# First and last tile: four products in full precision, nine unread products at a norm, and a new written order

## The chip, the cores and the metric

The kernel runs on one core of one Trainium2 chip. The metric is the device time of one execution in microseconds (us). TensorE is called PE, VectorE DVE, ScalarE ACT, GpSimd POOL and SyncE SP. SP issues almost all the DMA transfers here. "Granted clock" is the share of full speed that the chip's throttle allows PE, as the profile records it.

## The reference, cut to what matters

The input x is 32 sequences of 256 tokens of 128 features. Two layers follow each other; each is `x = x + s(xn) * silu(f(xn))` with `xn = layernorm(x)`.

```python
xs = jnp.pad(x, ((0, 0), (1, 0), (0, 0)))[:, :-1]        # first layer, s
xm = x * time_mix + xs * (1.0 - time_mix)
k = jnp.exp(jnp.minimum(jnp.einsum('btc,dc->bdt', xm, Wk), 60.0))
v = jnp.einsum('btc,dc->bdt', xm, Wv)
r = jnp.einsum('btc,dc->btd', xm, Wr)
wkv = _depthwise_causal_conv(k * v, w, T, C)             # decaying sums over time
wk = _depthwise_causal_conv(k, w, T, C) + 1e-09
s = jnp.einsum('btc,dc->btd', jax.nn.sigmoid(r) * (wkv / wk), Wo)
```

Beside it, the first layer's gate `f` is three products with weights of +1 and -1 (128 to 512 to 512 to 128 features) with relu. The second layer's `s` is a state space block (projection, convolution over 4 tokens, scan), and its `f` is a mixture of 2 shared and 16 routed experts with the 4 best weighted by a router.

## The kernel before

The tokens are cut into 16 tiles of 512 (two whole sequences each), named 0 to 15 (in base 36, 0 to f, in the written order). A tile lies as 128 features by 512 tokens. About two tiles are in flight at a time, the first layer of one beside the second layer of the tile before.

**Products.** Nearly all PE products are made from two rounded parts. A value is copied into a rounded type (fp32r) as its high part (`hi_of`, an ACT copy or activation), the rest is subtracted out as the low part (`lo_of`, on DVE or POOL), and `mm3` (L636) adds three products, high by high, low weight by high, and high weight by low. Weights are split once, by `halves` and in `w_o`. An unrounded product of fp32 operands is one call and becomes two passes through PE; the seven last `down` products of each tile are of this kind (tile `pm`, weight `w_n`).

**One tile's first layer.** `norm0` gives `xn`; `part0` splits it (`x1`); `mix` makes `xm` with DVE and splits it (`xm0h` by ACT, `xm0l` by POOL for tile 0). `key`, `kv` and `recept` multiply it by three of the four weights in `wkvro` (tiles `pk`, `pv`, `pr`). `quot` (L876) divides the two sums, multiplies by the gate `tr`, and splits the result (`z0h` by ACT, `z0l` by DVE). `back` (L910) multiplies by the output weight `w_o` (tile `po`), by the gate `g` of the signed products (`sign0`, `sign1`, `sign2`: tiles `pha`, `phb`, `pz`), adds onto `xr` and transposes to `pt`. `norm1` (L932) takes the statistics of `pt` on DVE (`bsb`, `mvb`), the power on POOL, normalises four blocks (`xnb`), transposes each back on PE (`psb`), and splits the result into `x2`, for tile 0 `x20h` and `x20l`. All of the second layer reads `x2`: `conv` and `res` (`pi`, `pres`), the router's `logits` (`pl`, eight small products), and `up` (`pu`).

**At the start** `warm` (L491) issues 14 products of a constant of ones, `wm`, whose results nothing reads, between the loads and the first transposes.

**What sets the order.** Every step is a generator; one step usually issues one instruction. `ORDER` (L160) is a string of three characters a step, the tile and the number of the part, and `run` (L334) takes the steps in that order. It thus fixes the sequence of every engine's queue, SP's DMA queue too; each queue is worked in sequence, with waits on semaphores. `SLOTS` (L106) says which buffer each new tile takes. PSUM has 8 banks, tag `psq`, one for each product tile.

Of the kernel before, what the change touches and what calls it, by code (L numbers as in the profile page):

```python
# [16 lines left out]
P = 128  # L17
# [3 lines left out]
NJ = NTOK // P  # L21
# [21 lines left out]
N1D = ()  # L43
NCV = 2
# [7 lines left out]
WARM = 14  # L52
WV = (1,)
# [54 lines left out]
        '0123045678250312530171120573663507222367502257603220367566275301132570002713511573207735201330152711'  # L108
        '357206635027117026535263170'
    ),  # L110
    'bs': '00000101110000011111101000000000',
# [4 lines left out]
        '0123401221043210301243011043210424013240043210433104231001324103031423011023410220143201120341021204'  # L116
        '3120102341022103421001243103'
    ),
    'h': (
        '012341056789abc5147603ac167459b82def9f2d5fe89417cb6a30gd48ac84d7g23b9f51915fb193604827gdca4cag8c54d7'  # L120
        '2063bf9171736190afb42d8g5cb8b248c5gd71a963f07d63d7g849b25c0fa1b99c5b48d3f6g71a02a20172ag639fd85c4be4'
        'f3c53f90ga21674ff47624fa8b19g05c3e1b1c5b2697f48ae30gdb3d0ed345g8f679c18c96cba817f05dg416'
# [3 lines left out]
    'md': '00000000000000',  # L126
    'mr': '0123032330203020032303030332',
    'mt': '00000000000000',
    'mv': '01111020345512202334455112225555',
    'pb': '0000000000000000',  # L130
    'psq': (
        '0123410532610762151760432154257262016421360403546030127013755147531650250435453743502615376542325635'
        '5753521073136243242133567061627674711474103462732241025402151603761476713733521354075716274030762700'
        '4561460135170171251324756562403123012105370657246247120643475127161340041041556237265737431704011604'
        '2056241673213723576060417245472522043734110723756356236247104323156315753653271534161721672027526342'
        '6405161501767261530175276374267743035134723640622474501664673701272140251706307130235045041507620543'
        '7316236723023754745104604303663025467375102130252312413657025302164301037637441270463527141026134571'
        '0012572743160732457347563'
    ),
    'rest': '0000000000000000',  # L140
    'rs': '01101010101010100101100110010110',
# [3 lines left out]
        '0120201210331200456721389046509183462920504382631594807461390470825a23481018973273991307128628531064'  # L145
        'a15037951a05430697341a87260489a3b0b63649623b0961257a3498c6892a756c68657a60b836a79543a584b890a3589c20'
        'b7240b5373b025053b78a504a2b580738b403a7283c9c4a09538c4537907c389405a6943ca2b65c4539b6935c2ab53c9b738'
        'a4c9057ba9874830b4a97b33b0296875920b657b989075a842b7653c1616c518474b42714812b0220021847b58451058501b'
    ),
    've': '0011111000000001000110111111111111',  # L150
    'wk': '00000000000000000000000000000000',
    'x2': '01100110011001100110011001100123',
    'xi': '01101010011001100110011010010110',
    'xna': '00',
    'xr': '0123454012354012',
# [5 lines left out]
g0pg0pg0pg0pg0p000g0hg0fg0pg0fg0fg0fg0fg00g0fg07g08g01100g0pg03002002002g0pg0fg0fg0gg0gg0hg04002g0og0o002g0g002002002g0g  # L161
g0g002g0ig0i002002002102102102g0jg0j102102102102102102g02g0gg0ag09g0cg0fg0fg0fg0m002g0k002002g0b002002102002002200002g0q
g0f102004g0fg0mg0d003008005102g0q102004102g0j003g0l005008004g0eg0kg0og05g0kg0fg0f102004102102006006102102102005300g0vg06
005007007008g0j00800e00e00e10100g00g00600g00e009006g0j00e00900900700700e00f00fg0j10300i00i00i00i00a00a00a00a00a00a00900a
00a00a10300900900900920220220220220220210510500g201g0v00f20220200b00b00b00b00900900h301g0l40100140000cg0t00cg0t20200c00c
00c00c00c20200c00j10600h106g0u00j00b00a00b00b00b00h202g0l00j00bg0r00b00j10820220200cg0u00cg0r10510510710720200d00dg0tg0t
g0t108g0sg0t109109106202302g0s10700j00d00d00d30210400j10c00d30210810c00d30250030230230230230210400j00d00k30200j00l00l109
10600l40210a30210c40220200l00l10c30210730210910430210a10410a10910810cg0ng0n10910c50240210e10e40270040240240240230200l00l
00l50240210c00m00l00m10c10c10e00m00m00m00m00m00m00m10i10i10e00m10910910a50250260040210a50250250250210a10a10a10e00m50210e
10a00m00m00m00m00m00m00m00m00n10f10f20210i109g0n50200m10f20400n00o20300n30210j10900q00n00q10c00q00q00q00q00q00o00q01s01s  # L170
01s10j60200q00n20360200o01k60201k00q60201k80060260200q60260201100r01s10j60201101101860210i00r00n01801800r00r00r30201k00n
01o01c00r00r01c70201o00r00r10a01100r01801c01o01470200r01410g01100r10g01o00r00r01gg0ng0n10g00o01110b01c01400r00r00n00o01g
01g70200u70200r10g10b01410b70270270270270200u00r01g90000u70210b00o00t00t10h00t10d01510b00n01901d00o10b00n10b10h00n10b10d
10d10d01l00u01p01w00o10b01001w10h01w01000o00o00o10b01001001030310d10d01601310d10d10j00t10j00p01601h01630401a00p00p10k00p
01301380201e01701720620680200p10j01080201t01780210j01x00p01ma0001b20610j10l10l20401q10l10l00s00z00z00z00s00s00w01f00w10l
00v20420820601i00v00z00z10l00z00y00y10l10l01u20880210l80280280201w10m10m20701j20700y10m20710m20520500x00x10m10m10m20501n
01y10m10m01020801r01v20701020801z10m20502040201020i20410m20i20e20940240280290200x80210m10m40220920e90210m10m20i20i10m10m
20e90210m40220920e10m20c90220910m902902902902209209c0010o10n20e10o10n00z90220c902a0210n00za02a02a0220e00z10q10qb0010q10q
10q10q30320f10q20f10q20f10o10n20950102120910o20a20a20c40210o20a02110n10q10q10q10n20j10r20j02102120c40220c20c20c10r10r20c
02102120c20a11802120a20911820j40311802111811120c11111111c10r20911c11c11c40411k10r10o10r10r20a40311k02111o11o11k10r11o10r  # L180
11k10r10o20a20a10r11o10r11g11110r11g11g10r11s10r10n11g11s11s10r10o11411411120g20g10r20g20a11111410r11s20b10n11420b20b115
20g10t20b11d20b20a20b20b20h11310n10n10n20b11911320h20b11l10t10t10u10u10u20h20b20d20d20d20d20d11610o10o10z10z10z10o11311t
10t11p20j11e10p11620j10u11w10p10p20j10p20d20d11w20d10p11611h20j11a11x11w20k11711711011020j20l20l20l10p11m11711w20l305305
30810s11b30530420l10s10s10z10w308305110110110a02a02a02a0211q10w30420l10v10y10y11i10v20l20l20l30e11f30820m30e20m30630610y
10x10x10z11y11010z50230811j50250230620m11u110502307307307a0230611n50220m20m20m20m20m20m11011r30720m11011vb0230420mb02b02
b0211z10x120a0220m20m30id0030i30930i30920m20m60120m20m20m30i30e30930e30a30a10z30e40410z10z30e30f30f20m50230c40430a30f30a
30930930c30930930c30c30c30930c12150230930c30c12120n20m12112120n30j12112130c20n30920o30c30j20o20n20o30a12120n20q20q20q20q
20q20q20q12120q21120o20q21121120q30j20o30a20q21k30a30a20n20r20r20r20r21k12140421o21o21k21s20r21c21k20o21s21s21o21121c21c
20o21s21g21c20r21g20r21820r20r20n20r21821121821420r21821420r20r21g20r21421130a30g30g21g30g20r21o30b30a20r30b30b20o20r214
30b30b30g30b20r21w21321w30b20n30h21321320o20o20t21520t20t30h20o21w21d20n20n30b30d30h20n21930d21l20t30d30d30j21t30j21030b  # L190
21030b30j20u50450330d20u20u21021021030d30d30j21630d21e21020u21h30j30l30l21630k40640621a21p30l30l40620z21x20z20z21640620p
21720p20p20p21720z20z30l20p21721b21m30l20p21i30l30l21u20s30l30m30m20w30m30m21f21j20s20s20w21q30m30m30m30m30m20y20y20v405
40520v21n21r30mc02c02405c0240521w40720y20x40760220x21y21v602602407b02602b02b02b02408c0240i40i20z210e0040821z40i407b02b02
21030m22060221040i20x40e70140930m30m40e40e30m30m30m30m40930m20z40840c40940e50430m30m20z20z40a40a40e40e60240c40c409408409
40940c40940c40c22122160240c40f40f40c40f40a40940c40a30o40922130o50422122122130n22150440j40a30n40j30n40940c30n30q30q30q221
30q30q30q30q30q30o40a40a30q30n40a30q30q30o30r40j30n30r30r30r31850322131c31c31831831c31131831131130n31k30o30r31o31o31o31c
31130r30r31k31k31k30r30r30n30r31s31s31s30r30r31430r30r31430o31431131g31o31g30r31g31131s40g40g40a30r40g30r30o31w31w31g40a
30r31w31440b40b40g40b40b31530o40b40b40b30t30n30n40b31d30n30t31331930t31l31330o30o40h30o31p31340d40h40d40d40d40b40h40j30u
# [98 lines left out]
def recurrent_d2(  # L297
# [439 lines left out]
    def mix(i):  # L737
# [18 lines left out]
        yield  # L756
        nc.scalar.copy(hi_of(s, "m", f"xm{i}", "xmp"), xm)
        yield
        lo_of(s, "m", f"xm{i}", "xmp", xm, "gpsimd")


    def sign0(i, m_):
# [169 lines left out]
    def norm1(i):  # L932
# [10 lines left out]
        for j in range(NJ):  # L943
# [10 lines left out]
            if j == 0:  # L954
                ps = bank([P, NJ, P], f"psb{i}", "psn")
# [427 lines left out]
```

## Time and profile before

| | us |
|---|---|
| three runs | 659.71, 660.61, 661.27; median 660.61 |
| the profiled execution | 659.82 |
| its span, first to last instruction | 658.0 |
| PE busy in the span | 641.4 |
| DVE busy | 572.2 |
| ACT busy | 549.3 |
| POOL busy | 384.0 |

The profile shows one execution. Its page gives the busy time of each engine and 40 slices of the span; the trace behind it can be asked for the instructions of an engine in order of time, for busy time in any stretch, and for the chain of waits that ended last. A number in square brackets at an instruction is the time its engine idled before it, with what ended the wait. Matmuls are pipelined, so that the distance of their starts, not their listed length, is what one costs.

### The profile page before, as it was taken

The page shows a single profiled execution, that of the slowest core. Times are in us where ns is not written, and L with a number is a line of the kernel's source. Part 1 is how long each engine was busy: PE and PEld are TensorE (multiplying, and loading weights), DVE is VectorE, ACT ScalarE, POOL GpSimd, SP SyncE. Part 2 cuts the span into 40 slices and gives each one's busy share as a digit, 9 for nine tenths or more (in the row PEclk, how much of TensorE's full clock was granted, in tenths as well). Part 3 has the DMA queues.
Part 4 walks back from the last instruction along what each step waited for, and adds up shares of the span by engine and source line. Part 5 has one row for each costly group of instructions (what it writes and reads, how often), then busy time and mean ns, then how long its engine had stood idle before and what let it go on. Part 6 is the DMA issues. An engine that isn't in the chain of part 4 may idle for free.

```text
span 658.0 us, 8819 instructions
## 1 busy us (share of the span) xinstructions
PE 641.4 (97%) x2626; PEld 461.5 (70%) x2626; DVE 572.2 (87%) x1364; ACT 549.3 (83%) x911; POOL 384.0 (58%) x398
## 2 busy tenths in 40 slices
PE   8999999999999999999999999999999999999997
PEld 6667676876757777576777767677675876767664
DVE  5989999979988899888888988988888798979886
ACT  8969797878969879797888979889797997967984
POOL 6585848567392773828466393944738374262542
PEclk9979999999999999999999999999999999999999
DMA  7334223142230413204132220413123040310431
GB/s 239 138 80 142 69 84 113 64 130 65 93 103 32 137 59 114 65 24 144 43 132 65 87 91 30 133 49 130 47 71 110 17 130 12 91 46 0 146 94 69
DMA packets 43648, 57.38 MB, mean 87 GB/s; under 512 B 3936, under 2 KB 20432, under 8 KB 43600
## 3 DMA queue, kind: packets, MB, share of 16 engines
q1 hardware_dynamic: 43456, 56.80, 26.9%
q8 instruction: 21, 0.34, 0.2%
q14 instruction: 27, 0.22, 0.1%
q10 hardware_dynamic: 144, 0.01, 0.0%
HBM read 52.02 MB, written 4.78 MB: 86 GB/s over the span
## 4 chain that ended last, share of the span: by engine, by line
PE 78%; DVE 11%; ACT 6%; issue 2%; DMA 2%; POOL 1%; SPq 0%; DVEq 0%; ACTq 0%
PE phb L634 15%; PE pm L634 14%; PE pu L634 13%; PE pc L634 6%; PE pha L634 4%; PE pz L634 3%; PE pi L634 3%; PE py L634 3%; PE pres L634 3%; PE pp L634 2%; PE po L634 2%; PE pk L634 2%; PE pl L634 2%; PE pv L634 1%; ACT L410 1%
## 5 line engine op out<-in xcount | busy, mean ns | idle before, releaser
L414 POOL TENSOR_TENSOR act<-act,ge 128x512 f32<-128x512 f32 x109 | 139.2, 1301 | 19.3 <-DMA ge<-gd 14.7
L410 ACT ACT_TABLE_LOAD x99 | 127.0, 1283 | 2.8 <-PEq L1371 1.2
L634 PE MATMUL pm<-act,w_n 128*128 128x512 f32 x224 | 106.0, 592 | 0.0
L417 DVE SCALAR_TENSOR_TENSOR pi<-xiz,par_sb,pi 128x512 f32<-128x512 f32 x96 | 70.4, 744 | 1.0 <-ACT pi L976 0.7
L414 POOL TENSOR_TENSOR xc_0l<-y,xc_0h 128x512 fp32r<-128x512 f32 x15 | 19.4, 1296 | 85.0 <-ACT y L411 64.3
L634 PEld LDWEIGHTS pm<-act,w_n 128*128 128x128 f32 x224 | 41.8, 189 | 29.9 <-issue 23.5
L411 ACT ACTIVATE act<-pu 128x512 f32<-128x512 f32 x109 | 61.2, 601 | 1.2 <-PE pu L634 0.3
L414 POOL TENSOR_TENSOR y<-y,rs 128x512 f32<-128x512 f32 x30 | 38.3, 1278 | 18.7 <-DVE y L1122 18.1
L1122 DVE TENSOR_TENSOR_SCAN y<-pd,y 128x256 f32<-128x256 f32 x64 | 39.9, 669 | 4.4 <-ACT pd L411 4.1
L414 POOL TENSOR_TENSOR xr<-gm,xr 128x512 f32<-128x512 f32 x15 | 19.3, 1288 | 30.1 <-DVE gm L414 25.1
L634 PE MATMUL phb<-ha_0h,w 128*128 128x512 f32 x64 | 27.3, 431 | 0.1
L1056 POOL MEMSET m<- 128x16 f32 x16 | 1.8, 112 | 43.7 <-DVE m L1054 43.7
L634 PE MATMUL phb<-ha_0l,w 128*128 128x512 f32 x64 | 26.1, 410 | 0.0
L634 PE MATMUL phb<-ha_2h,w 128*128 128x512 f32 x64 | 25.6, 403 | 0.0
L634 PE MATMUL phb<-ha_1h,w 128*128 128x512 f32 x64 | 25.5, 401 | 0.0
L634 PE MATMUL phb<-ha_3h,w 128*128 128x512 f32 x64 | 25.5, 398 | 0.0
L411 ACT ACTIVATE pd<-pd 128x512 f32<-128x512 f32 x32 | 17.9, 581 | 9.0 <-PE pd L634 8.8
L634 PE MATMUL phb<-ha_3l,w 128*128 128x512 f32 x64 | 25.3, 396 | 0.0
L634 PE MATMUL phb<-ha_2l,w 128*128 128x512 f32 x64 | 25.2, 397 | 0.0
L952 DVE TENSOR_SCALAR xnb<-pt,mvb 128x128 f32<-128x128 f32 x64 | 22.8, 401 | 2.3 <-POOL mvb L669 2.2
L634 PE MATMUL phb<-ha_1l,w 128*128 128x512 f32 x64 | 24.7, 396 | 0.0
L414 POOL TENSOR_TENSOR xc_1l<-y,xc_1h 128x512 fp32r<-128x512 f32 x15 | 19.4, 1296 | 8.7 <-ACT y L411 8.7
(1160 smaller groups left out, 2201.9 us busy)
## 6 DMA issues: line engine op xcount, KB each, us to landing
ge<-gd SPq DMA_DIRECT2D x128, 256.0 KB
mra<-mda SPq DMA_DIRECT2D x28, 256.0 KB
xt<-in_x SPq DMA_DIRECT2D x16, 256.0 KB
xr<-in_xr SPq DMA_DIRECT2D x16, 256.0 KB
out_x<-xr SPq DMA_DIRECT2D x16, 256.0 KB
w_up<-in_w_up SPq DMA_DIRECT2D x3, 192.0 KB
gd<-gT SPq DMA_DIRECT2D x16, 32.0 KB
w_n<-in_w_down SPq DMA_DIRECT2D x1, 448.0 KB
```

The lines of the kernel that those rows point to most:

```text
L410: nc.scalar.preload_act_table_set(SETS[kinds[0]])
L411: nc.scalar.activation(*args, **kw)
L414: getattr(nc, engine).tensor_tensor(o, a, b, op)
L417: nc.vector.scalar_tensor_tensor(o, a, s, b, op0, op1)
L634: nc.tensor.matmul(ps, lhsT=w, rhs=r, start=start, stop=stop)
L952: nc.vector.tensor_scalar(xn[:, j, :], s["pt"][:, j, :], mv[:, j, 0:1], r, ALU.subtract, ALU.mult)
L1056: nc.gpsimd.memset(m8[:, :, TOPK:8], -1.0)
L1122: nc.vector.tensor_tensor_scan(y[:, tok], sp[:, tok], y[:, tok], 0.0, ALU.mult, ALU.add)
```

## The change

For tiles 0 and 15 (`NAT`), `xm` and the quotient are no longer split: `key`, `kv`, `recept` and `back` make one product each from the unrounded values and the unrounded weights, where they made three. `wkvro` gets a place of its own, as it is read to the end. In `norm1` of tile 0, nine products of the constant `wm` are added, 128 by 128 by 128, into the bank of `psb`, read by nothing: six ahead of the four transposes and one after each of the first three.

`ORDER` and `SLOTS` are written anew from the first character to the last. Read out by queue, the new order differs from the old most in the first tile:

- SP: the first seven loads are `k0`, `xt` of tiles 0 and 1, `k2`, `w_dt`, `k1`, `wkvro` (before: `xt` of tile 0, `w_dt`, `w_rt`, `k0`, `xt` of tile 1, `wkvro`, `k2`).
- PE: 13 of the 14 unread products stand ahead of the first transpose (before 10); of the six new ones, one stands ahead of and five behind the last four `phb` products of tile 1 that come ahead of `norm1`'s transposes.
- ACT: the copy `w_k_h` moves from ahead of tile 0's first use of `psa` to behind its third relu; `w_c_h` moves from ahead of the gate `g0` to behind it; one more table load in the whole kernel (100, before 99).
- DVE: two subtractions and products of small constants (`w_r`, `cs`) move from the start to between two steps of tile 0's quotient; `ha1_1l`, `ha1_2l` and `xm1` stand between the quotient and `g0`.
- POOL: `w_c_l` moves from ahead of tile 0's `xr` addition to just ahead of the power in `norm1` of tile 0; two small weight steps (`w_p`) move from there to behind.

In the middle tiles the queues hold the same steps in nearly the same sequence, with neighbours exchanged. PE's queue still closes with tile 15's seven unsplit `down` products and the six `py`; between `pd15_0`, which tile 15's last scan waits for, and these stand two split `down` products (before, these two and two `pc`).

```diff
+NAT = (0, 15)
...
+WARM2 = 6
...
     def w_o(i):
-        w = cst("w_o", (P, P))
+        ready["w_of"] = w = cst("w_o", (P, P))
...
             stt(seqs(xm), seqs(xn), col(MIX), t1[:, :, 0:T], ALU.mult, ALU.add)
+        if i in NAT:
+            s["m"] = xm
+            return
         yield
         nc.scalar.copy(hi_of(s, "m", f"xm{i}", "xmp"), xm)
         yield
         lo_of(s, "m", f"xm{i}", "xmp", xm, "gpsimd")
+
+    def kvr(i, ps, k):
+
+        if i in NAT:
+            mm(ps, raw["wkvro"][:, k, :], st[i]["m"])
+        else:
+            w = ready["w_k"]
+            yield from mm3(lambda: ps, (w[0][:, k], w[1][:, k]), lambda: st[i]["m"])
...
-        yield ["mix", "w_k"]
+        yield ["mix", "get_wkvro" if i in NAT else "w_k"]
         pk = bank([P, NTOK], f"pk{i}", "pk")
-        yield from mm3(lambda: pk, (w[0][:, 0], w[1][:, 0]), lambda: s["m"])
+        yield from kvr(i, pk, 0)
...
         yield ["recept"]
-        if POC:
+        if POC and i not in NAT:
             stt(pv, s["tr"], 1.0, pv, ALU.add, ALU.mult)
...
-        if POC:
+        if POC and i not in NAT:
             w = ready["w_o"]
             yield from mm3(lambda: po, w, lambda: s["z"])
         else:
-            mm(po, ready["w_o"], s["tr"])
+            mm(po, ready["w_of"], s["tr"])
...
+        for k in range(WARM2 if i == 0 else 0):
+            yield
+            if k == 0:
+                ps = bank([P, NJ, P], f"psb{i}", "psn")
+            mm(ps[:, NJ - 1, :], wm[:, 0:P], wm[:, 0:P])
         for j in range(NJ):
...
             nc.tensor.transpose(ps[:, j, :], xn[:, j, :], ident)
+            if WARM2 and i == 0 and j < NJ - 1:
+                yield
+                mm(ps[:, NJ - 1, :], wm[:, 0:P], wm[:, 0:P])
...
-        ("wkvro", [P, 4, P], wkvro, "raw"),
+        ("wkvro", [P, 4, P], wkvro, None if NAT else "raw"),
```

## Prediction

> **What bounds the kernel now.** I read the page first, then busy time by stretch, PE's instructions in order of time around the slow slice, and the chain of waits at both ends.
>
> ```profile
> PE 641.4 (97%) x2626; PEld 461.5 (70%) x2626; DVE 572.2 (87%) x1364; ACT 549.3 (83%) x911; POOL 384.0 (58%) x398
> ...
> PE   8999999999999999999999999999999999999997
> ...
> PEclk9979999999999999999999999999999999999999
> ```
>
> PE is full in 38 of 40 slices, so a microsecond of PE work or of PE idling is about a microsecond of time. One slice, the third, has a low granted clock. By stretch (columns: PE, PEld, DVE, ACT, POOL busy, clock):
>
> ```profile
> 25.00:41.50 16.50, 13.74 (x55) 8.85 (x54) 15.42 (x52) 12.76 (x25) 14.83 (x19) 1.00 0.40 114
> 41.70:48.50 6.80, 6.80 (x21) 5.64 (x21) 5.19 (x18) 5.04 (x9) 4.75 (x6) 0.50 0.07 12
> 46.00:100.00 54.00, 53.08 (x217) 38.79 (x217) 52.88 (x148) 47.14 (x81) 33.06 (x36) 0.98 0.32 102
> 100.00:580.00 480.00, 475.65 (x1979) 345.42 (x1978) 421.20 (x968) 408.76 (x671) 287.34 (x268) 1.00 0.26 82
> 580.00:653.50 73.50, 71.95 (x277) 47.58 (x275) 61.53 (x141) 54.77 (x87) 31.55 (x31) 1.00 0.20 66
> ```
>
> For 6.80 us the clock is 0.50: 3.4 us of PE work are lost there. But from 46 to 100 us DVE is nearly as full as PE (52.88 of 54.00), so what PE wins early DVE need not follow. From 100 to 580 PE idles 4.35 us, to 653.5 another 1.55. PE at the fall of the clock:
>
> ```profile
> 38.79 0.40 PE L634 MATMUL phb<-ha_3l,w 128*128 128x512 f32 x1
> 39.54 1.28 PE L956 MATMUL psb<-ident,xnb 128*128 128x128 f32 x4 [0.35 <-DVE xnb L952]
> 41.50 0.67 PE L634 MATMUL pi<-x20h,w_i_h 128*128 128x512 f32 x1 [0.68 <-ACT x20h L959]
> ...
> 48.36 0.46 PE L634 MATMUL pu<-x20l,w_u_h 128*128 128x512 f32 x1
> 48.66 0.40 PE L634 MATMUL pu<-x20h,w_u_h 128*128 128x512 f32 x1
> ```
>
> Between 39.03 (0.24 after the start of the last `phb`) and 41.50 PE has four short transposes and nothing else, the second norm of tile 0. Then products start 0.43 us apart instead of 0.23, until 48.5. Five instructions of other engines in order of time, which the steps below use:
>
> ```profile
> 32.32 0.69 ACT L411 ACTIVATE g<-pz,cs 128x512 f32<-128x512 f32 x1
> 33.81 1.29 POOL L414 TENSOR_TENSOR xr<-xr,g 128x512 f32<-128x512 f32 x1 [0.26 <-DVE g L414]
> 37.72 0.19 POOL L667 TENSOR_SCALAR veb<-mvb 128x4 f32<-128x4 f32 x1 [0.41 <-DVE mvb L664]
> 45.85 0.29 DVE L1027 TENSOR_REDUCE lg<-pl 128x64 f32<-128x128 f32 x1 [1.61 <-PE pl L634]
> 48.75 1.37 DVE L1049 TENSOR_TENSOR pb<-lg,tot 128x64 f32<-128x64 f32 x1
> ```
>
> The chain of waits near its end (start, length, what):
>
> ```profile
> 646.04 6.01 PE pm L634 x14
> 652.04 1.41 PE py L634 x6
> ```
>
> DVE stood 1.61 us for the slow router products, and ACT 1.48 us behind it. In the chain, a pass of an unrounded product (`pm`) costs 6.01/14 = 0.43 us, and PE works without a gap up to the last `py`.
>
> **The change part by part.** The sum is made against the profiled execution, 659.82 us (span 658.0), which lies inside the three runs and 0.79 under their median 660.61; I carry the difference over to the median.
>
> *Four products.* Three rounded products cost 3 x 0.233 = 0.70 us of PE, one unrounded product 2 x 0.43 = 0.86: +0.16 each, +0.64 for a tile. Per tile two ACT copies of 0.5 us (`xm0h`, `z0h`), a POOL subtraction (`xm0l`, 1.35) and a DVE one (`z0l`, 0.60) go. In tile 0 PE idles 2.76 us between 25 and 41.5, so its +0.64 is taken as covered (without that cover, +0.64).
>
> *The way to tile 0's second norm.* From 10 to 31 us ACT is full, and its chain is what ends last. In front of `g0` the new queue loses `xm0h` (0.51, by the distance of the starts), `z0h` (0.57) and `w_c_h` (0.52), and gains `w_k_h` (0.40), which was issued earlier: 1.2 less. The start gives a little back: `k0` is loaded ahead of tile 0's `xt`, one issue of 0.47 us later, and the first weight chunk `w1` (0.71) stands ahead of `x10h` where `w_k_h` and `t1z` (0.40 and 0.58) stood. So `g0` starts about 1.1 earlier than 32.32. DVE's `g` follows it (it waited 0.32 for ACT before) as `z0l` is gone, and so does POOL's `xr`. On POOL `w_c_l` (1.29) now queues ahead of `veb`, and the norm waits behind it; but 0.74 of `w_p` has left that place, and 0.41 was idle: 0.14 later. The normalised blocks then come 1.0 us earlier.
>
> *w_r and cs on DVE's quotient chain.* They hold no more than 0.2 us, unless POOL reads SBUF then. The `pb` product above took 1.37 while POOL ran a 1.30 subtraction from the same moment, and the same instruction took 0.22 at 560.66; `cs` itself took 1.23 beside `xm0l`. So this move costs 0 to 1.0 us each; I take 0.3 for both, since DVE's `g` has 0.32 of waiting to lose first and half of POOL's work there is small.
> The Trainium skill (SBUF — State Buffer, "Who interferes with whom") has the rule behind it: a DVE instruction with both inputs in SBUF contends with a POOL instruction that reads SBUF, and the later one blocks for the whole of it. It speaks against putting these two there; by it both would block, about 2 us on this chain.
>
> *Nine unread products.* No row has them: two passes each of 128 columns. A 256-column pass of `pw` costs 0.21 us warm (4 in 0.79 of weight loads), an unrounded weight load 0.19, a transposing pass 0.11. So 0.22 to 0.38 each, 2.0 to 3.4 us in all. The gap they fill was 0.51 ahead of the first transpose, 0.2 after each of three, 0.68 before `pi`. PE reaches the five behind the last `phb` about 1.1 us earlier than before, if the chain above holds; they take 1.1 to 1.9, and delay the first transpose by 0 to 0.3 against the new `xnb`; each of the three between adds 0 to 0.2. Bounds for this edit: 0 to +1.9 (no lead at all and the upper price). I take +0.4, near the lower end since the lead is the likelier case. Together, `x20h` comes 0.3 to 0.4 us earlier (bounds: 1.1 earlier, 1.4 later).
>
> *The clock.* The new products put 2.0 us or more into a gap of 2.5. Between 24.5 and 27.9 us PE was idle for about 1 of 3.4 us and the clock stayed at 1.00; after the last product, at 653.43, it fell 3.1 us later. So with two thirds of the gap filled I expect it to stay. The low time, 6.8 us, is twice 3.4; the window in which it fell held 0.7 us of products and four transposes.
> The Trainium skill (TensorE: Matmul & The Clock Gate, Part 1) asks for a whole idle window of about 3.4 us before the clock is halved, which by itself would make the nine products needless, as no idle time here was over 0.7 us. Part 4 of the page adds that transposes do not count as busy, which would leave 2.5 us idle. By the page's rule alone the clock should not have fallen; the row shows that it did, and the row decides.
>
> What that is worth: PE's 3.4 us at most. But the router's way is x20l (ends 42.13), one `pi` and eight `pl` at full clock (0.23 + 0.80): 43.2, while DVE has `pk`, `hb_0l`, `hb_3l` and one `bsa` to do until 44.25. So `lg` comes forward by the 1.61 that DVE waited, and the stretch to 100 us, which DVE fills, by 1.6; DVE's remaining 1.1 us of idling there could add up to 0.8. I take -1.6 (bounds 0 and -3.4), plus the -0.3 of the way there: **-1.9**. What is late next is DVE.
>
> *Tile 15.* PE is full, so +0.64; but its norm chain left PE idle 1.13 us between 580 and 612, and it loses `z15h` and `z15l` (1.1 us). Bounds -0.5 to +0.64; I take **+0.2**.
>
> *The order.* In the middle the queues hold the same sequence with neighbours exchanged, and SP's gate loads too. PE idles 4.35 us there; half of that more or less is ±2. One more ACT table load is 1.28 us of an engine with 17% to spare. I take **0**. At the end PE's closing stretch after `pd15_0` is 0.23 + 0.47 + 6.01 + 1.17 before the last `py`: 7.9 us, against 7.2 that softplus, scans and `yy` took there from 644.86 to 652.1. It stays covered.
>
> Sum: -1.9 + 0.2 + 0 = **-1.7**. The profiled execution would be 658.1, the median **658.9** us.
>
> **The rivals.**
> *The clock falls anyway (slower).* The new quotient leaves PE idle between 25 and 31 us (it waited 0.84 and 0.62 before), and the unread products come too late or too short. For: 0.7 us of products in a window did not hold it. Against: the first unread products held the clock at 1.00 from the start. Then the 3.4 us stay lost, the nine products stand on the norm's way (+1.9 at the upper end, less 1.1 of lead), and tile 15 adds 0.64: +1.4, **662.0** us. It decides as soon as the granted clock around 42 us is 0.50.
> *DVE or a bank takes it all (no change).* The clock stays, but DVE meets POOL's reads in the quotient (+1.0 to 2.0), and later the order loses what is left: -1.9 + 1.5 + 0.2, **660.4** us. For: DVE's 52.88 of 54.00.
> *More is kept.* The whole 3.4 us and 0.8 of the way: about **656.6** us, if the new order has moved DVE work out of 46 to 100 us, where ACT and POOL have room.
>
> **How the numbers follow.** 0.2% is 1.3 us, about what a measurement of this kernel can tell from no change. Forecast 0.45 (657.6 to 660.0), more kept 0.15, no change 0.2, slower 0.2 (the clock case and an order that costs 2 us in the middle). Faster by more than 0.2% means under 659.3: most of the forecast, all of the third rival, 0.58. Same 0.2, slower 0.22. The range leaves out one tenth at each end: 656.3 to 662.0.
>
> **What would show it.** Right: clock 1.00 from 40 to 50 us, `lg` of tile 0 near 44 instead of 45.85, `g0` near 31.3, the third slice of PEclk at 9. PE's idle time from 100 to 580 near 4.4. Wrong: a 0.50 anywhere in 38 to 50, transposes of `psb` that start late behind the unread products, `w_r` or `cs` at over 1 us, or `pt` of tile 15 waiting longer than before.

## The result, and the profile after

The changed kernel is slower: 663.63 us, the median of six runs (661.92 to 664.03), against 660.75 for the kernel before (six runs). The ratio is 1.0040, 95% interval 1.0026 to 1.0055, which is 2.6 us. The forecast was 658.9 with a range of 656.3 to 662.0. The profiled execution of the changed kernel took 662.92 us (span 661.1). Below, kernels are compared by their ratio to the kernel before, run beside them on the same chip; 0.001 of it is 0.66 us.

The page of the changed kernel, its busy times, PE's row and the clock's row:

```profile
PE 645.3 (98%) x2636; PEld 459.1 (69%) x2636; DVE 569.7 (86%) x1362; ACT 548.4 (83%) x908; POOL 380.2 (58%) x396
...
PE   8999999999999999999999999999999999999997
...
PEclk9899999999999999999999999999999999999999
```

PE's busy time rose by 3.9 us, more than the span did (3.1). The dip of the clock has moved from the third slice to the second. Busy time by stretch (PE, PEld, DVE, ACT, POOL, then the clock), to be laid beside the rows of before:

```profile
25.00:41.50 16.50, 14.48 (x54) 9.95 (x53) 13.51 (x47) 11.59 (x22) 12.88 (x15) 0.90 0.33 98
41.70:48.50 6.80, 6.12 (x42) 5.34 (x41) 6.76 (x22) 5.33 (x11) 5.83 (x6) 1.00 0.11 39
46.00:100.00 54.00, 53.69 (x228) 39.14 (x227) 52.49 (x151) 48.81 (x84) 36.05 (x41) 1.00 0.32 104
100.00:580.00 480.00, 475.30 (x1961) 340.46 (x1960) 418.88 (x963) 405.93 (x668) 282.20 (x265) 1.00 0.25 81
```

The clock is at 1.00 where it was at 0.50, from 41.7 to 48.5, and from 46 to 100 us PE takes 228 instructions where it took 217. That part of the forecast came true in this execution. The loss shows in the last row, and it shows in the count more than in the busy time: from 100 to 580 us PE idles 4.70 us (before 4.35), but it takes 1961 instructions where it took 1979.

The end did what was forecast. In the chain of waits near its end (start, length, what), PE again works without a gap from `pm` to the last `py`:

```profile
648.71 6.47 PE pm L635 x16
655.18 1.40 PE py L635 x6
```

The way to tile 0's second norm did not. These are DVE, ACT and POOL instructions of the changed kernel in order of time; where an engine idled before one, the idle time and what ended it stand in brackets:

```profile
27.46 0.70 DVE L562 TENSOR_TENSOR w_r<-raw_w_rt,w_r 128x16 fp32r<-128x16 f32 x1
...
32.72 0.69 ACT L412 ACTIVATE g<-pz,cs 128x512 f32<-128x512 f32 x1 [0.24 <-PE pz L635]
...
38.31 1.28 POOL L415 TENSOR_TENSOR w_c_l<-w_x,w_c_h 128x512 fp32r<-128x512 f32 x1
40.32 0.20 POOL L668 TENSOR_SCALAR veb<-mvb 128x4 f32<-128x4 f32 x1 [0.73 <-DVE mvb L665]
...
43.99 0.59 ACT L977 CAST x20h<-psb 128x512 fp32r<-128x512 f32 x1 [1.47 <-PE psb L971]
...
47.12 0.29 DVE L1045 TENSOR_REDUCE lg<-pl 128x64 f32<-128x128 f32 x1
```

`g0` starts at 32.72, not at the 31.2 of the forecast. Only 0.24 us of that is a wait for PE's `pz`: the table load ahead of it on ACT ended at 32.48, and tile 0's first exponential, `kt`, had started 1.6 us later than before (17.59, before 15.97). `veb` comes 2.6 us later than before, and `x20h` at 43.99 where it had been at 40.86. From there the full clock wins 1.9 us back: `lg` is 1.3 later than before, not 3.1. Why `pz` was late shows in PE's instructions in order of time:

```profile
27.69 0.47 PE L635 MATMUL phb<-ha_0h,w 128*128 128x512 f32 x1 [0.91 <-DVE hb_2l L418]
...
28.89 0.50 PE L635 MATMUL phb<-ha_0l,w 128*128 128x512 f32 x1 [0.50 <-DVE ha_0l L418]
...
29.49 0.63 PE L635 MATMUL pz<-hb_0l,w 128*128 128x512 f32 x1
29.92 0.63 PE L635 MATMUL pz<-hb_1h,w 128*128 128x512 f32 x1
```

PE started five products between 26.2 and 29.4 us. There the clock fell to 0.50, until 32.8, and PE ran seven of the eight `pz` products at a distance of 0.43 us instead of 0.23: the clock had fallen earlier than in the kernel before, at the quotient.

By PE's own ledger (the distance of each start to the next, less what such an instruction takes in full flow) the added work is 3.2 us, 8 x 0.16 for the unsplit products and 18 x 0.107 for the unread ones, and the excess over it is 35.1 us in both kernels. It fell by 2.9 us up to 100 us and by 1.2 behind 580, and rose by 4.0 between. This looks as if the added work had simply been added, which is one theory; that the order lost in the middle what it had won at the start is another. The experiments tell them apart.

### The profile page after: what moved, and what is told of

It reads as the page before. It is cut to its first block, busy times and chain, and to the rows that moved or that the text cites. A ratio compares the mean times of both kernels' runs of the same rounds, so it can differ in the third digit from the quotient of the medians.

```text
span 661.1 us, 8827 instructions
## 1 busy us (share of the span) xinstructions
PE 645.3 (98%) x2636; PEld 459.1 (69%) x2636; DVE 569.7 (86%) x1362; ACT 548.4 (83%) x908; POOL 380.2 (58%) x396
## 4 chain that ended last, share of the span: by engine, by line
PE 79%; DVE 9%; ACT 8%; issue 2%; DMA 1%; SPq 1%; POOL 1%; DVEq 0%; ACTq 0%; POOLq 0%
PE phb L635 15%; PE pm L635 14%; PE pu L635 12%; PE pc L635 6%; PE pz L635 4%; PE pha L635 4%; PE py L635 3%; PE pres L635 3%; PE pi L635 3%; PE pp L635 2%; ACT L411 2%; PE po L635 2%; PE pk L635 2%; PE pl L635 1%; ACT act L412 1%
## 5 line engine op out<-in xcount | busy, mean ns | idle before, releaser
L635 PE MATMUL phb<-ha_0h,w 128*128 128x512 f32 x64 | 28.9, 454 | 1.0 <-DVE hb_2l L418 0.9
L415 POOL TENSOR_TENSOR xr<-xr,g 128x512 f32<-128x512 f32 x15 | 19.8, 1320 | 10.6 <-DVE g L415 10.6
L994 ACT ACTIVATE pi<-pi,par_sb 128x512 f32<-128x512 f32 x32 | 24.0, 754 | 0.5
```

The lines of the kernel that those rows point to most:

```text
L415: getattr(nc, engine).tensor_tensor(o, a, b, op)
L635: nc.tensor.matmul(ps, lhsT=w, rhs=r, start=start, stop=stop)
L994: nc.scalar.activation(pi, pi, AF.Identity, bias=col(CONVB + h), scale=col(cw + 3))
```

## The experiments

The written order is a sequence of steps, so two orders can be joined: the steps of one up to some point, then the steps that are left in the sequence of the other. Buffers were carried over with the part that they belong to. "Old" is the order of before without the steps that fall away.

| kernel | start / tiles 5 to 11 / end | unsplit | unread | ratio to before, 95% | us |
|---|---|---|---|---|---|
| after | new / new / new | 0, 15 | yes | 1.0040 (1.0026 to 1.0055) | +2.6 |
| e1 | old / old / old | 0, 15 | yes | 1.0031 (1.0017 to 1.0045) | +2.0 |
| e2 | old / old / old | none | yes | 0.9992 (0.9977 to 1.0007) | -0.5 |
| e3 | old / old / old | 0, 15 | no | 1.0027 (1.0012 to 1.0042) | +1.8 |
| e4 | new / new / new | 0, 15 | no | 1.0057 (1.0036 to 1.0078) | +3.8 |
| e5 | old / old / old | 0 | yes | 1.0004 (0.9992 to 1.0016) | +0.3 |
| e6 | old / old / old | 15 | yes | 1.0017 (1.0004 to 1.0030) | +1.1 |
| e7 | old / new / new | 0, 15 | yes | 1.0046 (1.0029 to 1.0064) | +3.0 |
| e8 | new / old / old | 0, 15 | yes | 1.0006 (0.9996 to 1.0017) | +0.4 |
| e9 | new / old / old | 0 | yes | 0.9985 (0.9972 to 0.9997) | -1.0 |
| e10 | new / old / old | none | yes | 1.0028 (1.0011 to 1.0045) | +1.8 |
| e11 | new, one step moved | 0, 15 | yes | 1.0052 (1.0032 to 1.0072) | +3.4 |
| e12 | new / new / new | 0 | yes | 1.0053 (1.0033 to 1.0073) | +3.5 |
| e13 | new / old / new | 0, 15 | yes | 0.9979 (0.9968 to 0.9991) | -1.4 |
| e14 | new to tile 8, then old | 0, 15 | yes | 1.0036 (1.0024 to 1.0048) | +2.4 |
| e15 | old / old / new | 0, 15 | yes | 0.9997 (0.9985 to 1.0008) | -0.2 |
| e16 | new, other PSUM banks | 0, 15 | yes | 1.0044 (1.0029 to 1.0058) | +2.9 |
| e17 | e13, other PSUM banks | 0, 15 | yes | 1.0004 (0.9989 to 1.0019) | +0.3 |
| e18 | new, one table load less | 0, 15 | yes | 1.0066 (1.0046 to 1.0085) | +4.4 |

### The edits apart from the order: e1, e2, e3, e4

```diff
 e1: ORDER, SLOTS: those of before, without the steps that fall away,
     and with nine steps of norm1 of tile 0 added
 e2: as e1, and
-NAT = (0, 15)
+NAT = ()
 e3: as e1 without the nine steps, and
-WARM2 = 6
+WARM2 = 0
 e4: the new ORDER without the nine steps, and
-WARM2 = 6
+WARM2 = 0
```

> The written order of before, with both edits of the work in it: four unsplit products in tiles 0 and 15 (the steps that fall away are struck out of the order) and the nine unread products (six ahead of tile 0's first psb transpose, one behind each of the first three). Theory 'order': the new order loses some 4 us between 100 and 580 us and the edits are worth what was forecast; then this kernel is at 659.0 us, 1.7 under before. Theory 'work': PE is the bound, and all PE work that the edits add shows (8 x 0.16 for the unsplit products, 18 passes of 0.107 for the unread ones, 3.2 us), whatever the order; then 663.9 us, as after. Theory 'clock': the gain hangs on where the clock falls; 659 with a granted clock of 1.00 from 40 to 50 us, 662 or more without.

> Before with the nine unread products alone, in the order of before. 'Order': the clock stays at 1.00 from 40 to 50 us, and the 1.6 us that the clock was put at come in, less up to 0.4 for the products' place on the norm's way: 659.0 to 659.5. 'Work': 18 x 0.107 = 1.9 us more PE work, 662.6. 'Clock': 659 if no slice near 41 to 48 us is at 0.50, 661 to 662.5 if one is.

> Before with the four unsplit products of tiles 0 and 15 alone, in the order of before. 'Order': the tile 0 products are covered and tile 15 costs 0.2; ACT loses two copies ahead of g0, so 660.0 to 661.0 with the low clock of before still there. 'Work': 8 x 0.16 = 1.3 us more, 662.0. 'Clock': as before, 660.7, the low clock moved by no more than 1 us.

> After without the nine unread products, its order otherwise. 'Order': the loss of the middle stays, so 663.0 or more, and 664 to 665 if the clock falls at tile 0's second norm without them. 'Work': 1.9 us less than after, 661.7. 'Clock': 663.6 if the low clock lies at 29 to 33 us as in after, since nothing before that time changes.

Measured: e1 662.31 us, e2 660.00, e3 661.65, e4 664.12, before 660.40. No theory fits all four. "Order" misses e1 by more than 3 us: the edits by themselves, in the old order, already cost 2.0 us. "Work" fits e3 (1.3 for a measured 1.8) and is 1.2 too high for e1, but it misses e2: the unread products add 1.9 us of PE work and make the kernel no slower. They hold the clock, as a stretch of e2's profile shows (columns as above):

```profile
41.70:48.50 6.80, 5.72 (x28) 4.38 (x28) 6.20 (x20) 6.65 (x12) 5.70 (x8) 1.00 0.17 39
```

The runs show besides how often the clock falls and what that costs. The kernel before was timed in 142 runs whose clock is listed: in 46 of them the mean granted clock is 0.991 to 0.996, in the other 96 it is 0.998 to 1.000. The means are 660.93 and 659.61 us. The fall thus costs 1.32 us (standard error 0.18), close to the 1.6 of the forecast, but it happens in a third of the runs; the profile that the forecast was read from, at 0.993, was one of that third. With the old start and the unread products (e1, e2, e5, e6, e7, e15), 4 of 65 runs are below 0.998, all of them e5's. So the edit is worth about 0.4 us on the mean. With the new start and the unread products (after, e8 to e14, e16 to e18) it is 48 of 106 runs; in the six profiles of these kernels that show a fall, one lies at the quotient, between 28 and 35 us, ahead of the unread products (e10 has another at 14 us). The new start thus brings a fall of its own, which they can't hold off.

e4 says the same from the other side: without the unread products the new order is 1.1 us slower than after (intervals overlapping), all six runs are below 0.998, and its profile has the fall behind tile 0's second norm, from 44.1 to 50.9 us.

### Which tile, and which half of the order: e5, e6, e7, e8

```diff
 e5: as e1, and
-NAT = (0, 15)
+NAT = (0,)
 e6: as e1, and
-NAT = (0, 15)
+NAT = (15,)
 e7: ORDER: old up to the first py of tile 5, then new
 e8: ORDER: new up to the first py of tile 5, then old
```

> The order of before with the nine unread products and unsplit products in tile 0 only. Its base is the kernel with the unread products alone, 660.0 us, whose clock never fell; both edits together stood at 662.3. Theory 'work': tile 0's four products add their 0.64 of PE and nothing covers it, 660.6. Theory 'cover', that of the prediction: PE idles in tile 0's first stage, so nothing is added, 660.0. Theory 'tile 0': the whole 2.3 us come from here, because tile 0's chain has no lead to lose, 662.3.

> The order of before with the nine unread products and unsplit products in tile 15 only. Base 660.0. 'Work': 0.64 more, 660.6. 'Cover': the forecast's +0.2, 660.2. 'Tile 15': the profiled kernels with unsplit products lost 1.2 to 1.4 us between 545 and 596 us, so this tile carries most of the loss, 661.3 to 662.0.

> All edits; the order of before up to the first py of tile 5 (about 280 us), and the new order from there on, the steps already taken left out. Base: all edits in the old order, 662.3. Theory 'middle': the new order loses its time between 340 and 440 us, so this kernel has the loss whole, 664.5 to 666. Theory 'start': the new order's loss is its start (tile 0's second norm 3 us later), and its rest is even with the old one, 662.3 or less.

> All edits; the new order up to the first py of tile 5, and the order of before from there on. 'Middle': without the stretch from 340 to 440 us of the new order, 661 to 662. 'Start': 663.5, as after.

Measured: e5 660.23 us, e6 661.18, e7 662.82, e8 660.09, before 659.78. Against e2, tile 0's unsplit products cost 0.8 us, near their 0.64 of PE ("work"), and tile 15's cost 1.7, more than twice their work. The two add up to e1. The traces don't put all of this at the edits. By the starts of the same PE instructions, e5 is 0.4 us behind e2 up to 100 us and 1.8 from 130 us on: between them, at 126 us, DVE is held up in the steps of a later tile (the race in the last section). e6 loses 1.1 us at the same place and 0.9 behind 560 us. e2's twelve times stand in two groups, 657.81 to 659.59 and 660.42 to 661.05, so prices taken against its median are rough.

Then the order: e8 is 1.7 us faster than e1, so the new start gains, although its `x20h` starts later than e1's (43.34, e1 42.27); and e7 is 1.0 slower than e1, so the rest of the new order loses. "Middle" was right in direction, though e7 fell short of its figure. Where the start gains is seen in DVE's rows, first e1, then e8:

```profile
157.52 1.75 DVE L418 SCALAR_TENSOR_TENSOR xm<-mra,par_sb,t1z 128x512 f32<-128x512 f32 x1
```

```profile
156.56 0.74 DVE L418 SCALAR_TENSOR_TENSOR xm<-mra,par_sb,t1z 128x512 f32<-128x512 f32 x1
```

The same PE instructions of e8 start 1.1 us behind e1 at 40 us and 1.4 ahead of it at 200, with steps of 0.75 to 1.0 us at 126, 158 and 194 us. At these three places e1's DVE takes 1.3 to 1.8 us for a `lg` or `xm` while POOL works, and e8's takes 0.2 or 0.7. From 40 to 200 us e1 has seven such rows of over 1 us, e8 one (e5 eight, e9 one). That these steps are the gain fits their sum; no run has tested it.

### A better kernel, and the longest wait: e9, e10, e11, e12

```diff
 e9: as e8, and
-NAT = (0, 15)
+NAT = (0,)
 e10: as e9, with tile 0's split steps put directly behind what they split, and
-NAT = (0,)
+NAT = ()
 e11: the new ORDER, with the first product of pha10_2 (a07) moved behind pt9's transposes
-a0681x81fa0781w80y
+a0681x81f81w80y
...
-c0290l80x80x81j
+c0290la0780x80x81j
 e12: the new ORDER with tile 15's split steps put directly behind what they split, and
-NAT = (0, 15)
+NAT = (0,)
```

> The new order up to the first py of tile 5, the order of before from there on; nine unread products; unsplit products in tile 0 only. Theory 'sum': the parts add up. With tile 15 unsplit as well it stood 0.4 us above before, and tile 15's unsplit products cost 1.6 (661.18 less 660.0, with the ratios' bases), so this kernel is 1.2 under before. Theory 'same': tile 15's loss is made up elsewhere when the start is early, so no change against the kernel with both tiles, 0.4 above before.

> As the last, but with split products in tile 0 too (the copies and subtractions put directly behind the values that they split, and the split of the first layer's weights ahead of tile 0's use of them): new start, old rest, nine unread products, nothing unsplit. 'Work': tile 0's unsplit products cost their 0.64 of PE, and this kernel is 0.6 faster than the last, 1.8 under before. 'Chain': in the new start ACT has no room for the copies, so it is 0.5 to 1 slower than the last, 0.2 to 0.7 under before.

> After with one step moved: the first product of pha10_2 goes from just ahead of tile 9's transposes pt9 to just behind them, and the two tiles exchange PSUM banks from there on, so that pt9 follows psb_8 (read early) and not pd8_1 (read by tile 8's scan, 0.9 us after the sum is ready and later). Theory 'bank': the wait of 1.97 us at pt9 goes, and 1 to 2 us with it: 661.6 to 662.6. Theory 'elsewhere': DVE or ACT are what is late there, the wait turns up again within 20 us, 663.3 or more.

> After with tile 15's four products split again (copies and subtractions directly behind the values that they split), tile 0 unsplit. 'Tile 15': the 1.6 us found in the old order come back here too, 662.0. 'Made for it': the new order's last stretch is laid out for unsplit products, so nothing comes back, 663.6.

Measured: e9 659.32 us, e10 661.81, e11 663.73, e12 663.69, before 660.62. e9 beats the kernel before, by 1.0 us. e10 is 2.8 us worse than e9, more than "chain" had. Two instructions of ACT show why, first e9, then e10:

```profile
17.57 0.62 ACT L413 ACTIVATE kt<-pk 128x512 f32<-128x512 f32 x1
...
43.95 0.59 ACT L978 CAST x20h<-psb 128x512 fp32r<-128x512 f32 x1 [1.47 <-PE psb L972]
```

```profile
19.47 0.59 ACT L413 ACTIVATE kt<-pk 128x512 f32<-128x512 f32 x1
...
45.99 0.59 ACT L978 CAST x20h<-psb 128x512 fp32r<-128x512 f32 x1 [1.49 <-PE psb L972]
```

The copies of the weights and of `xm0` that split products need hold tile 0's first product `pk` 1.2 us back (14.44, e9 13.27) and its first exponential 1.9, and the delay stays whole to `x20h`. In this execution of e10 a fall of the clock from 14.3 to 17.7 us adds to it; but in the runs without a fall the two kernels also stand 2.8 us apart (means 661.55 and 658.78). So tile 0's unsplit products cost 0.8 us where the order was made for split ones, and are worth 2.8 us where it was made for them. This price holds for the places that I gave the copies; better ones were not tried.

e11 took away the longest wait of the middle. In the changed kernel it looks so, first PE, then DVE:

```profile
385.47 0.80 PE L635 MATMUL pha<-x110h,w 128*128 128x512 f32 x1
387.67 0.41 PE L938 MATMUL pt<-ident,xr 128*128 128x128 f32 x2 [1.41 <-DVE y L1140]
...
384.86 1.48 DVE L418 SCALAR_TENSOR_TENSOR xm<-mra,par_sb,t1z 128x512 f32<-128x512 f32 x1
386.27 1.26 DVE L1140 TENSOR_TENSOR_SCAN y<-pd,y 128x256 f32<-128x256 f32 x2
```

`pha10_2` had been exchanged with `pt9` and took the PSUM bank that became free early; `pt9` had to wait for the bank of `pd8_1`, which tile 8's scan reads, and the scan queued behind `xm11` on DVE, which took 1.48 us beside POOL's products where the median `xm` of e13 takes 0.74. In e11 PE shows this:

```profile
385.15 0.38 PE L938 MATMUL pt<-ident,xr 128*128 128x128 f32 x2
386.69 0.27 PE L685 MATMUL pmva<-ident,mva 128*8 128x128 f32 x1 [1.15 <-ACT act L412]
...
387.44 0.50 PE L635 MATMUL pha<-x110h,w 128*128 128x512 f32 x1 [0.37 <-DVE ha_1l L418]
```

`pt9` starts 1.8 us earlier (2.5, less 0.7 that this execution was ahead), and the next taker of a bank, `pmva12`, waits instead, for a gelu behind a table load, and `pha10_0` after it: 1.15 and 0.37 for 1.41. The time did not move. "Elsewhere" holds: at this place moving the wait to another tile made no difference.

e12 gave nothing either (3.5 above before, after 2.6): where the end was laid out for unsplit products, splitting them again gains nothing.

### Where the new order gains and loses: e13, e14, e15

```diff
 e13: ORDER: new up to the first py of tile 5, old to the first py of tile 11, then new
 e14: ORDER: new up to the first py of tile 8, then old
 e15: ORDER: old up to the first py of tile 11, then new
```

> All edits; the new order up to the first py of tile 5, the order of before from there to the first py of tile 11 (about 515 us), the new order from there on. Theory 'own gain': the last stretch of the new order is 2 us better by itself (it is laid out for tile 15's unsplit products), so this kernel is 2 us faster than the one with the old order to the end, which stood 0.4 above before: 1.6 under before. Theory 'catching up': the new order only regains there what DVE and ACT had in hand because PE was late, so this kernel is 0.4 above before.

> All edits; the new order up to the first py of tile 8 (about 400 us), the order of before from there on. 'Early': the loss begins at 330 us and holds most of its sum by 400 (2.5 of 4 in the profiles), so 1.5 to 2.5 us above the kernel that changes at tile 5, 2 to 3 above before. 'Late or given back': what is lost to 400 us is regained later under the old order, under 1 us above before.

> All edits; the order of before up to the first py of tile 11, the new order from there on. Base: all edits in the old order, 2.0 above before. 'Own gain': 2 us less, even with before. 'Catching up': 2.0 above before.

Measured: e13 659.42 us, e14 663.15, e15 660.62, before 660.70. "Own gain" holds twice, with the new start (e13 against e8, -1.8) and with the old one (e15 against e1, -2.2). "Early" holds: e14 has 2.0 us of loss against e8. e13 is all of the change but for the middle of the order, and it is the fastest kernel of this study, 1.4 us under before (interval 0.6 to 2.1; e9 lies inside it). The change as it was made differs from e13 in the order of tiles 5 to 11 alone, and in the buffers that go with it, and that costs 4.0 us (about 2.8 to 5.2, the two intervals taken as independent). With the old start the same exchange, e7 against e15, costs 3.2. Busy time from 340 to 460 us, the changed kernel first, then e13:

```profile
340.00:460.00 120.00, 117.40 (x482) 83.57 (x482) 103.70 (x229) 100.20 (x165) 68.14 (x63) 1.00 0.25 78
```

```profile
340.00:460.00 120.00, 119.47 (x499) 86.88 (x499) 105.35 (x234) 104.47 (x171) 70.98 (x65) 1.00 0.27 85
```

In the same 120 us PE takes 17 instructions fewer, and no engine is fuller in exchange: DVE and ACT, the next busiest, lose busy time too. So it is waiting, and not more work. Start of the same PE instruction less its start in e13, both counted from the first PE instruction (median of each 20 us):

```
from us   280   340   380   420   500   600   640
after    0.44  1.38  2.76  4.07  4.36  4.46  3.50
e14      0.19  1.11  2.41  2.40  2.48  3.47  3.87
e8      -0.40 -0.40 -0.40 -0.44 -0.41  0.53  0.65
```

Each round of a tile from 8 to 11 loses about a microsecond; e14 stops losing when it changes to the old order.

### Banks and the table load: e16, e17, e18

```diff
 e16: the new ORDER; SLOTS['psq']: each product tile takes the bank whose last use lies furthest back
 e17: e13's ORDER; SLOTS['psq'] in the same way
 e18: the new ORDER, tile 6: gelu of act6_8 (61w) moved behind the softplus of pd6_0 (60v)
-70l61f61w60s60s61061q80660y60y60v61j
+70l61f60s60s61061q80660y60y60v61w61j
```

> After, its order untouched; each of the 625 product tiles takes the PSUM bank whose last use lies furthest back in the order (408 tiles follow another tile than before). Theory 'banks': the new SLOTS are what makes PE wait in the middle, so 2 us or more come in, 661.5 or less, with the wait at pt9 gone. Theory 'sequence': any choice of banks meets the same full PSUM, since the steps that would free a bank are late; 663 to 664.5.

> The kernel with the new order in the first and last tiles and the old one from tile 5 to 11, banks chosen in the same way. 'Banks': the choice matters in general, so this one moves by 1 us or more, most likely up from 659.4. 'Sequence': within 0.7 us of 659.4.

> After with the gelu of tile 6's last up product (act6_8) moved behind the softplus of pd6_0, so that ACT loads 99 tables and not 100. Theory 'table': the load of 1.28 us on ACT, 91% busy from 300 to 340 us, starts the loss that follows, so 1 us or more comes in, 662.6 or less. Theory 'sequence': the load lies in ACT's slack and the loss begins only at 330 us in tile 8's steps, 663 to 664.5.

Measured: e16 662.89 us and e17 660.54 with before at 659.76, e18 663.65 with before at 659.31. "Sequence" holds for e16, which stays at after's level with 408 of 625 tiles in other banks, and for e18. e17 sided with "banks": the choice was worth 1.7 us to e13 (intervals overlapping a little). So banks matter where the sequence is good, and the one other choice tried does not mend the other one. Which of the exchanged neighbours in tiles 5 to 11 start the loss stays open. So does the part of the SBUF buffers: in e13 they went with the order, and no run varies them alone.

## Why the prediction was wrong

*The order in the middle: 0, bounds ±2. Here it failed.* It measured +4.0. The working was that the queues hold the same steps with neighbours exchanged, and that PE's idle time there, 4.35 us, bounds what can change by half of it. Both halves are unsound. Nearly the same sequence is not the same time: e13 and after differ in the neighbours of tiles 5 to 11 and their buffers, and by 4.0 us. What in them costs it stays open. `pha10_2` and `pt9` had changed places, and PE stood 1.41 us there, but neither moving that wait (e11), nor other PSUM banks (e16), nor the table load (e18) brought the time back. And listed idle time is no bound: it went from 4.35 to 4.70 in the profiles, while the ledger of distances between starts rose by 4.0, as an instruction that waits within its listed length counts as busy (the `pha` at 385.47 is listed with 0.80, in full flow 0.40). The count of instructions in the stretch, 1979 to 1961, shows what the idle time hides.

*The clock: -1.6. The mechanism held where it was looked for, and the size was that of one execution.* The unread products hold the clock at 42 us, and a fall costs 1.3 us. But it falls in a third of the runs of before, so on the mean the term was 0.4. With the new start it falls at the quotient instead, in 48 of 106 runs; that gap the rival on the clock had named. Two readings in the working don't hold: the first seven passes of the unread products at the start stand 0.43 us and more apart, the later ones 0.22, so that by these distances the clock was not full from the first; and behind the last product it fell after 2.6 us, not 3.1.

*The way to `x20h`: 0.3 to 0.4 earlier. Wrong in sign, and in what it is worth.* It came 3.1 us later. ACT was 1.6 us behind at `kt`, and the copies that had gone from its queue only made that up: `g0` came 0.4 later, not 1.1 earlier. `w_r` met POOL and took 0.70 us where it had taken 0.20. PE, waiting at the quotient, lost its clock there, and DVE's `g` came 1.6 later. The four transposes `pt` then took 1.7 us from the first start to the last (before 0.9), so that `veb` came 2.6 later; it waited for `mvb`, not for `w_c_l` as forecast. The unread products added 0.5 for a forecast 0.4: from the first `xnb` to `x20h` it is 2.33 us, before 1.79. The fall of the clock is the smaller part: in the profiles of e8, e11, e12 and e16, with the same start and a clock of 1.00 there, `x20h` is still 1.7 to 2.6 later than before.

Yet the new start by itself gained 1.3 to 1.7 us (e9 against e5, e8 against e1). It is not that PE had more to do around this norm: from 25 to 41.5 us it was busy 14.33 us in e8 and 14.94 in e1. In the profiles the gain comes behind 100 us, where DVE is held up less often beside POOL.

*Tile 0's four products: covered, 0.64 if not.* 0.8 in the old order by the times (in the profiles 0.4 up to 100 us, and 1.1 more by the race at 126); in the new one they gain 2.8 against the placing of the copies that I tried. The forecast took the copies' absence as 1.2 us on ACT's way to `g0`; in e10, which has copies back, `kt` is 1.9 later, part of it by the clock.

*Tile 15: +0.2, bounds -0.5 to 0.64.* In the old order 1.4 to 1.8 (e6 against e2, e8 against e9, e1 against e5), outside the bounds (in the three pairs of profiles the stretch behind 560 us takes 0.9, 1.5 and 2.4 longer); with the new end around it, -0.4 (e13 against e9). I had not seen that the gain of an order made for the edit sits at the end of the kernel, 1.8 to 2.2 us.

*The tail: covered, 0.* Right.

By e2, e5 and e6 and the differences above: -0.5 for the unread products, +0.8 and +1.7 for tiles 0 and 15, -1.7 for the start, -1.8 for the end, +4.0 for the middle, together +2.5; measured +2.6. That this closes is no proof of the parts: start, end and middle are differences along one row of kernels that ends with the change itself, and only the first three terms, which give e1's 2.0, could have failed. Without the middle the sum is -1.5, and the forecast's was -1.7. That likeness is luck: the forecast had three to four times too much for the clock, almost nothing for tiles 0 and 15 (+2.5), and neither the gain at the start nor that at the end (-3.5).

No rival had this either. The one that ended slower put its loss on the clock, and in the new start, where the clock did fall, the runs with a fall are slower by 0.0 (e8), 0.5 (after) and 1.3 us (e13), not by 4. The chance for slower counted an order that costs 2 us in the middle, half of what it cost.

## What to carry to other kernels

When an order of steps is written anew, cost it by stretch: join old and new at a few points, and time each part by itself. Here the new order gains at both ends and loses more between, and neither edit nor order could be judged by the whole. When a profile shows a fall of the clock, ask in how many runs it falls before a price is put on it. And removing the longest wait of a stretch proves nothing until the time moves; if the resource behind it is full, the next in line waits. Before a gain or a loss is put down to an edit, look for instructions that took far longer than their like: a difference of 1 us can arise far from it, where two engines meet.

## What the runs showed of the hardware

*A race of 0.03 us that is worth 1.1.* e2 and e6 have the same queues up to tile 15, yet e6 loses 1.1 us at 126 us. DVE subtracts in the router (`lg`) while POOL subtracts `xm4l`. First e2, DVE and POOL:

```profile
125.54 0.21 DVE L1051 TENSOR_TENSOR lg<-lg,top 128x64 f32<-128x64 f32 x1
...
125.51 1.38 POOL L416 TENSOR_TENSOR xm4l<-xm,xm4h 128x512 fp32r<-128x512 f32 x1
```

```profile
125.84 1.35 DVE L1051 TENSOR_TENSOR lg<-lg,top 128x64 f32<-128x64 f32 x1
...
125.81 1.30 POOL L416 TENSOR_TENSOR xm4l<-xm,xm4h 128x512 fp32r<-128x512 f32 x1
```

In both POOL's instruction is listed 0.03 us ahead. In e2 DVE's takes 0.21 and POOL's 1.38; in e6 (second fence) DVE's takes 1.35 and POOL's 1.30. The Trainium skill (SBUF — State Buffer, "Who interferes with whom") calls the port pair that the two engines share an exclusive lock; the rows agree, and show that among starts 0.03 us apart either may get it. PE's starts in e6 lie 0.3 us behind e2 ahead of this place and 1.4 behind it. In the kernel before POOL is listed 0.02 ahead and DVE takes 0.21; in e1, e3, e5, e7 and e15, which share the old start with tile 0 unsplit, POOL is 0.06 to 0.08 ahead and DVE takes 1.29 to 1.31 in all five. So the edit in tile 0 may well decide a race nearly 100 us behind it; these are single profiles. At other places profiles of kernels with the same queues part in the same abrupt way (before and e2 by 0.8 us at 158 us and by 0.9 at 495); those were not followed up.

*A fall of the clock that varies from run to run.* In the profiled execution of before it fell at 41.7 us, and by the mean clocks about a third of the runs have a fall; in that of after it fell at 29.4 us and came back 3.4 us later. All falls between products in the profiles last 3.4 or 6.8 us. The Trainium skill (TensorE: Matmul & The Clock Gate, Part 1) says that the window in which the hardware judges PE's activity runs freely, so that the number of slow products varies from run to run; the 46 of 142 agree with that. Its condition of a whole idle window does not fit: five products started in the 3.4 us ahead of 29.4, and the longest idle time was 0.91 us.
